# A per-language adapter with residual and layer norm: every step of the plan gets its own key, and GpSimd copies some of the W1 tiles

## The chip, the cores and the metric

The kernel runs on one core of one Trainium2 chip. The metric is the device time of one execution in microseconds (us), the median of several runs. The engines of the core are named in the profile as PE (TensorE, matrix multiply), PEld (its weight load), DVE (VectorE), ACT (ScalarE), POOL (GpSimd) and SP (SyncE, which here only issues DMAs). An engine carries out its instructions strictly in the order in which the program lists them for it.

## The reference

`x` is 128 batches of 128 rows by 512 columns, float32. Each batch has a language number (`itok`, below 9 here, ten are provided for), which selects its matrices and vectors. For every batch:

```python
h       = relu(x @ W1[lang] + b1[lang])      # 128x512 @ 512x128
adapted = h @ W2[lang] + b2[lang]            # 128x128 @ 128x512
y       = x + adapted
normed  = (y - mean(y)) * rsqrt(var(y) + 1e-05)   # over the 512 columns
out     = x + normed * gamma[lang] + beta[lang]
```

## The kernel before

**One batch.** A batch is one tile of 128 partitions by 512 columns. Its steps, each a small function:

- `load_x(g)`, SP: the DMA of x for a group of four batches (`xp`, 4 buffers).
- `transpose_x(b)`, PE: four 128x128 transposes of x into one PSUM tile; `copy_xT(b)`, ACT: that tile to SBUF. For a batch of turn "F" four DMAs (`load_blocks`, SP) and one VectorE transpose (`turn_blocks`) do this instead, and W1 comes with four DMAs from HBM (`load_rows`).
- `stage_w1(b)`, ACT: copies the batch's W1 (128x512) out of a table of all languages in SBUF into a tile at a fixed place (`wp`, 7 buffers). For a batch of turn "w" a DMA fetches W1 from HBM by its number instead (`load_late`, SP).
- `down(b)`, PE: four matmuls with W1, recorded as eight instructions; `relu(b)`, ACT: adds b1; `up(b)`, PE: the matmul with W2 into a PSUM tile `y` (five buffers).
- `add_b2(b)`, POOL: r = x + b2 (`rp`, 4 buffers). It is there for batches of kind "P". For kind "E" there is none; instead `seed(b)`, ACT, copies x into the PSUM tile, and `up` adds onto it. For some early batches VectorE adds b2 (`vector_b2`).
- `add_beta(b)`, POOL: o = x + beta (`op`, 8 buffers for a pair of batches each).
- `residual(b)`, DVE: y = y + r with the row sums (y + b2 for "E"); `square(b)`, ACT: sum of squares about the mean; per pair of batches `scalar_means` and `deviation` on ACT and three `rstd` steps on DVE; `scale(b)`, DVE: (y - mean) * gamma; `finish(b)`, DVE: o = y * rstd + o; `store(g)`, SP: the DMA of a pair to HBM.

**The order.** `keep` ties each instruction to the one before it on its engine, so the order of the calls is the order of every queue. An opening (L605 to L644) and an epilogue for batches 116 to 127 (L708 to L858) are written out by hand. The opening ends with GpSimd's `add_beta` of batches 0 to 3. Between them stands the plan: L651 to L703 give every step a key, and L705 sorts by key and calls the steps. A key is the batch number plus an offset that is the same for all batches of a stage: `BATCH` and `PAIR` from batch 26 on, `BATCH_EDGE` and `EDGE` before it and in the last four batches, all in units of a batch. The epilogue begins on GpSimd with `b2_of(121)`, `b2_of(125)`, `beta_of(122)`, `beta_of(124)`, `b2_of(122)`, `beta_of(121)`, `b2_of(123)`, and on VectorE with `rstd` and `residual(119)`; E is 123.

`KINDS` and `TURNS` repeat every 16 batches: four of 16 are "E", two of 16 "F", one of 16 "w". Over the whole run ScalarE copies W1 91 times and seeds 24 times, and GpSimd does 206 adds in the plan (117 `add_beta` and 89 `add_b2`), after four in the opening.

Of the kernel before, what the change touches and what calls it, by code (L numbers as in the profile page):

```python
# [13 lines left out]
ET = mybir.EngineType  # L14
# [3 lines left out]
G = 4  # L18
EPS = 1e-5
FIRST = 17  # L20
EARLY = 17
LATE = 17
U = 2
MIDDLE = 26
TURNED = 32
LAST = 4
KINDS = 'EPPPPPEPEPPPEPPP'
TURNS = 'TTTTFTTTTwTTFTTT'
SEEDED = 'E'
ON_GPSIMD = 'P'  # L30
BATCH = dict(turn=0.19, copy=0.16, r=-0.36, beta=-0.13, relu=1.26, w1=-0.77, up=2.66, load=-5.59, r_late=0.22)
BATCH_EDGE = dict(copy=0.2, r=0.05, r_late=1.05, beta=1.06, relu=1.3, w1=-0.6, up=2.5)
SEED = {'E': 1.69}
PAIR = dict(stat=0.22, square=0.34, means=1.98, root=1.9, scale0=3.03, n1=2.43, n2=3.115, n3=3.28, scale1=3.4, end0=3.67, end1=4.32)
EDGE = dict(stat=0.6, square=0.68, means=1.75, root=1.77, scale0=2.64, n1=2.65, n2=3.592, n3=3.62, scale1=3.64, end0=3.66, end1=4.66)


@with_exitstack
def cond_resid_kernel(ctx: ExitStack, tc: tile.TileContext, x, itok, W1, b1, W2, b2, gamma, beta, out):
# [8 lines left out]
    nc = tc.nc  # L48
    B, S, H = x.shape
    L, _, A = W1.shape  # L50
    KC = H // P
# [27 lines left out]
    E = B - 5  # L79
# [6 lines left out]
    def xb(b):  # L86
        return xs[b // G][:, b % G, :]
# [5 lines left out]
    w1 = const.tile([P, L, KC, A], FP, name="w1")  # L93
# [34 lines left out]
    parts = const.tile([P, H], BF, name="parts")  # L128
# [14 lines left out]
    lids, w1s = {}, {}  # L143
# [8 lines left out]
    def lid(b, engine):  # L152
        g = b // G
        if (g, engine) not in lids:
            loads, vals = nc.values_load_multi_w_load_instructions(
                lang[0:1, g * G : (g + 1) * G],
                engines=[engine],
                min_val=0,
                max_val=L - 1,
                skip_runtime_bounds_check_because="clamped on the chip to 0..L-1 above",  # L160
            )
            for ins in loads:
                keep(ins)
            lids[g, engine] = vals
        return lids[g, engine][b % G]
# [95 lines left out]
    xT, hT, rs, os, ys, ssqs, nmeans, rstds = {}, {}, {}, {}, {}, {}, {}, {}  # L261
    phs, pxs, sums = {}, {}, {}


    def b2_by_matmul(b):
        return b in (0, 1) or b >= B - 2

    def kind(b):
        return KINDS[b % len(KINDS)] if MIDDLE <= b < B - LAST else "-"

    def turn(b):
        return TURNS[b % len(TURNS)] if TURNED <= b < B - LAST - 2 else "-"

    def seeded(b):
        return kind(b) in SEEDED

    def b2_on_gpsimd(b):
        return kind(b) in ON_GPSIMD or kind(b) == "-" and not b2_by_matmul(b) and not b2_by_vector(b)

    def b2_by_vector(b):  # L280
        return kind(b) == "-" and (b in (2, 3, 9, 13, 17, 21) or 24 <= b < B - 8 and (b % 16 in (1, 6, 11) or b % 32 == 30))

    x2s = {}

# [32 lines left out]

    def stage_w1(b):
        w1s[b] = wp.tile([P, KC, A], FP, tag="w1s", name=f"w1s_{b}")
        src = w1.rearrange("p l k a -> p (l k a)")[:, bass.ds(lid(b, ET.Activation) * (KC * A), KC * A)]  # L320
        keep(nc.scalar.copy(w1s[b].rearrange("p k a -> p (k a)"), src))  # L321

    def transpose_x(b):
        pxs[b] = p_x.tile([P, KC, P], FP, tag="xT", name=f"pxT_{b}")
# [16 lines left out]

    def add_beta(b):
        g, j = divmod(b, 2)
        if j == 0:
            os[g] = op.tile([P, 2, H], FP, tag="o", name=f"o_{g}")
        v = lid(b, ET.Pool)
        keep(nc.gpsimd.tensor_tensor(os[g][:, j, :], xb(b), beta_b[:, bass.ds(v * H, H)], ALU.add))  # L347
# [61 lines left out]
    def square(b):  # L409

        g, j = divmod(b, 2)
        if j == 0:
# [61 lines left out]
    def on(b):  # L474
        return 0 <= b < B
# [154 lines left out]
    spread(18, nc.scalar)  # L630
    spread(19, nc.scalar)
    add_beta(0)
    add_beta(1)
    spread(20, nc.scalar)
# [13 lines left out]
    def at(when, step, *args):  # L648
        plan.append((when, len(plan), step, args))

    for b in range(B):  # L651
        when = BATCH_EDGE if kind(b) == "-" else BATCH
        if b >= 20 and b % G == 0:
            at((11 if b == 20 else b - 7) - 0.01, load_x, b // G)
        if b >= 3:
            for n, engine in ((b + 5, ET.Activation), (b + 5, ET.PE), (b + 6, ET.Pool)):
                if on(n):
                    at(b + 0.99, lid, n, engine)
        if turn(b) in "Fw":
            at(b + BATCH["load"] - 1, lid, b, ET.SP)  # L660
            at(b + BATCH["load"], load_rows if turn(b) == "F" else load_late, b)
        if turn(b) == "F":
            at(b + BATCH["load"], load_blocks, b)
            at(b + BATCH["turn"], turn_blocks, b)
        elif 5 <= b <= E - 2:
            at(b, transpose_x, b)
            at(b + when["copy"], copy_xT, b)
        if 4 <= b <= E - 3:
            at(b + (when["r"] if seeded(b) else when["r_late"]), add_b2, b)
            at(b + when["beta"], add_beta, b)  # L670
            at(b + 1.1, down, b)
            at(b + when["relu"], relu, b)
        if seeded(b):
            at(b + SEED[kind(b)], seed, b)
        if FIRST <= b <= E - 1 and turn(b) not in "Fw":
            at(b + when["w1"], stage_w1, b)
        if 2 <= b <= E - 4:
            at(b + when["up"], up, b)
# [4 lines left out]
    def at_pair(g, when, step, *args):  # L683
        if g < E // 2 - 3 or (step, *args) in begun:
            at(2 * g + 3 + when, step, *args)

    for g in range(E // 2 - 1):
        b = 2 * g
        when = EDGE if "-" in (kind(b), kind(b + 2)) else PAIR
        for j in (0, 1):  # L690
            at_pair(g, j + when["stat"] - 0.01, vector_b2, b + j)
            at_pair(g, j + when["stat"], residual, b + j)
            at_pair(g, j + when["square"], square, b + j)
        at_pair(g, when["means"], scalar_means, g)
        at_pair(g, when["root"], deviation, g)
        if b % G == 0 and on(b + G):
            at_pair(g, when["end0"] + 0.001, lid, b + G, ET.DVE)
        for n in (1, 2, 3):
            at_pair(g, when[f"n{n}"], rstd, g, n)
        for j in (0, 1):  # L700
            at_pair(g, when[f"scale{j}"], scale, b + j)
            at_pair(g, when[f"end{j}"], finish, b + j)
        at_pair(g, when["end1"] + 0.001, store, g)  # L703

    for _, _, step, args in sorted(plan, key=lambda step: step[:2]):  # L705
        step(*args)
# [10 lines left out]
    copy_xT(E - 1)  # L717
    residual(E - 4)
    square(E - 4)
    rstd(E // 2 - 3, 3)  # L720
    relu(E - 2)
# [5 lines left out]
    end_of(E - 7)  # L727
    residual(E - 3)
    stage_w1(E)
    beta_of(E - 1)  # L730
    scalar_means(E // 2 - 2)
# [10 lines left out]
    relu(E - 1)  # L742
    down(E)
    stage_w1(E + 1)
    copy_xT(E + 1)
    transpose_x(E + 2)
# [149 lines left out]
```

## Time and profile before

| | |
|---|---|
| time, median of 3 runs | 300.57 us (300.26 to 300.83) |
| the profiled execution, its time | 301.23 us |
| the profiled execution, its span | 298.8 us |
| granted TensorE clock | 0.997 |

The span runs from the first to the last instruction that the profile shows; the time has some 2.4 us around it. In the profile's rows, a group's line names the source line, engine, operation, what is written and read by the program's names, and how often; behind the bar stand the busy time, the mean duration of one in ns, and idle time of the engine ahead of them with what ended it. In a timeline, a row's first number is the start and the second the length in us; rows that follow each other directly are merged (x2, x4). Busy time is a union, and on ScalarE, VectorE and GpSimd the next instruction starts a little before the last has ended, so a price per instruction is taken from start to start where that can be read.

### The profile page before, as it was taken

The numbers are of one execution on the slowest core, as the hardware profiler recorded it, in microseconds if no ns is written. First come the engines' busy times: TensorE is split into PE (matmuls) and PEld (weight loads), VectorE is DVE, ScalarE is ACT, GpSimd is POOL, SyncE is SP. The second block draws the span as 40 slices with busy tenths as digits, with TensorE's granted clock in tenths as the row PEclk, the third lists the DMA queues.
The fourth block names the chain that finished last, engine by engine and source line by source line (L and its number), as shares of the span: only waits on it lengthen the run. The fifth ranks groups of instructions, "written<-read, shape, count | busy, mean of one in ns | idle before, by whom it ended". The sixth has DMA issues, their size and how long they took to land.

```text
span 298.8 us, 7251 instructions
## 1 busy us (share of the span) xinstructions
PE 290.7 (97%) x1783; PEld 214.7 (72%) x1783; DVE 288.9 (97%) x775; ACT 277.2 (93%) x766; POOL 277.4 (93%) x233
## 2 busy tenths in 40 slices
PE   7899999999999999999999999999999999999993
PEld 3758777777777777777777777777777777777761
DVE  6989999999999999999999999999999999999995
ACT  5868789999999999999999999999999999999983
POOL 1299998999999999999999999999999999999962
PEclk9999999999999999999999999999999999999998
DMA  6999999996799697988888887898988698894715
GB/s 233 369 393 370 342 329 396 400 325 212 270 297 328 169 378 218 321 316 284 277 280 295 275 283 256 281 300 224 356 256 269 233 313 301 250 349 163 237 73 219
DMA packets 61195, 85.48 MB, mean 286 GB/s; under 512 B 3641, under 2 KB 25156, under 8 KB 61154
## 3 DMA queue, kind: packets, MB, share of 16 engines
q1 hardware_dynamic: 61094, 84.97, 85.1%
q8 instruction: 15, 0.25, 0.3%
q14 instruction: 26, 0.21, 0.2%
q10 hardware_dynamic: 60, 0.05, 0.1%
HBM read 51.45 MB, written 33.55 MB: 284 GB/s over the span
## 4 chain that ended last, share of the span: by engine, by line
PE 81%; DVE 6%; ACT 4%; DMA 3%; issue 3%; SPq 1%; DVEq 0%; POOL 0%; ACTq 0%; POOLq 0%
PE ph L353 33%; PE py L375 26%; PE pxT L330 15%; PE py L367 7%; DMA w<-in_L_cond_W_dram 3%; DVE py L393 2%; ACT sq L416 1%; DVE o L553 1%; DVE py L459 1%; ACT w1s L321 1%; ACT xT L334 1%; SPq L173 1%; DVE n L559 0%; ACT hT L361 0%; ACT root L426 0%
## 5 line engine op out<-in xcount | busy, mean ns | idle before, releaser
L347 POOL TENSOR_TENSOR o<-x,beta_b 128x512 f32<-128x512 f32 x121 | 155.8, 1306 | 12.9 <-DVE beta_b L259 11.6
L353 PE MATMUL ph<-xT,w1s 128*128 128x128 f32 x1024 | 136.4, 276 | 0.1
L353 PEld LDWEIGHTS ph<-xT,w1s 128*128 128x128 f32 x1024 | 125.0, 192 | 8.7 <-ACT hT L361 7.0
L340 POOL TENSOR_TENSOR r<-x,b_b 128x512 f32<-128x512 f32 x89 | 116.1, 1305 | 0.0
L375 PE MATMUL py<-w,hT 128*128 x208 | 106.7, 595 | 0.7 <-DMA w<-in_L_cond_W_dram 0.7
L330 PEld LDWEIGHTS pxT<-ident,x 128*128 128x128 f32 x468 | 60.4, 150 | 60.6 <-issue 41.6
L459 DVE SCALAR_TENSOR_TENSOR py<-py,nmean,gamma_b 128x512 f32<-128x512 f32 x124 | 93.3, 753 | 0.0
L468 DVE SCALAR_TENSOR_TENSOR o<-py,rstd,o 128x512 f32<-128x512 f32 x116 | 86.8, 748 | 0.0
L416 ACT ACTIVATE sq<-py,sum 128x512 f32<-128x512 f32 x124 | 85.6, 690 | 0.7 <-DVE rstd L435 0.2
L334 ACT COPY xT<-pxT 128x512 f32<-128x512 f32 x117 | 67.8, 580 | 6.0 <-PE pxT L330 5.8
L330 PE MATMUL pxT<-ident,x 128*128 128x128 f32 x468 | 71.2, 275 | 0.9 <-ACT gamma_b L244 0.7
L393 DVE SCALAR_TENSOR_TENSOR py<-py,r 128x512 f32<-128x512 f32 x94 | 64.9, 690 | 1.4
L321 ACT COPY w1s<-w 128x512 f32 x91 | 56.7, 623 | 0.0
L361 ACT ACTIVATE hT<-ph,b1T 128x128 f32<-128x128 f32 x128 | 47.6, 372 | 5.1 <-PE ph L353 3.4
L375 PEld LDWEIGHTS py<-w,hT 128*128 128x128 f32 x208 | 31.7, 192 | 2.1 <-DMA w<-in_L_cond_W_dram 1.2
L416 ACT ACTIVATION_READ_ACCUMULATOR sq<-py,sum 128x1 f32 x124 | 25.9, 209 | 0.0
L367 PE MATMUL py<-w,hT 128*128 x48 | 25.3, 610 | 0.0
L393 DVE SCALAR_TENSOR_TENSOR py<-py,b_b 128x512 f32<-128x512 f32 x24 | 16.6, 693 | 1.5 <-PE py L367 1.4
L426 ACT ACTIVATE root<-ssq,eps 128x2 f32<-128x2 f32 x62 | 16.5, 266 | 1.5
L316 ACT COPY py<-x 128x512 f32<-128x512 f32 x24 | 14.4, 599 | 0.0
L393 DVE DVE_READ_ACCUMULATOR py<-py,r 128x1 f32 x94 | 13.2, 140 | 0.0
L407 ACT ACTIVATE nmean<-sum 128x2 f32<-128x2 f32 x61 | 11.7, 192 | 0.0
(79 smaller groups left out, 139.8 us busy)
## 6 DMA issues: line engine op xcount, KB each, us to landing
out_dram<-o SPq DMA_DIRECT2D x62, 512.0 KB, 4.0
x<-in_x_dram SPq DMA_DIRECT2D x27, 1024.0 KB, 7.7
w1s<-in_L_cond_W_dram SPq DMA_DIRECT2D x26, 256.0 KB, 7.3
x<-in_x_dram SPq DMA_DIRECT2D x10, 512.0 KB, 6.0
w1s<-in_L_cond_W_dram SPq DMA_DIRECT2D x44, 64.0 KB, 3.2
x<-in_x_dram SPq DMA_DIRECT2D x44, 64.0 KB, 2.1
w<-in_L_cond_W_dram SPq DMA_DIRECT2D x4, 640.0 KB, 8.1
w<-in_L_cond_W_dram SPq DMA_DIRECT2D x1, 1792.0 KB, 10.2
```

The source lines that it names most:

```text
L321: keep(nc.scalar.copy(w1s[b].rearrange("p k a -> p (k a)"), src))
L330: keep(nc.tensor.transpose(pxs[b][:, k, :], cols, ident))
L334: keep(nc.scalar.copy(xT[b], pxs.pop(b)))
L340: keep(nc.gpsimd.tensor_tensor(rs[b], xb(b), b2_b[:, bass.ds(v * H, H)], ALU.add))
L347: keep(nc.gpsimd.tensor_tensor(os[g][:, j, :], xb(b), beta_b[:, bass.ds(v * H, H)], ALU.add))
L353: nc.tensor.matmul(phs[b], lhsT=w1s[b][:, k, :], rhs=xT_of(b, k), start=(k == 0), stop=(k == KC - 1))
L361: keep(nc.scalar.activation(hT[b], phs.pop(b), AF.Relu, bias=b1T[:, bass.ds(lid(b, ET.Activation), 1)]))
L375: keep(nc.tensor.matmul(ys[b], lhsT=hT[b], rhs=w2[:, bass.ds(v * H, H)], start=not m, stop=True))
L393: nc.vector.scalar_tensor_tensor(ys[b], ys[b], 1.0, r, ALU.mult, ALU.add, accum_out=sum_of(b))
L416: nc.scalar.activation(sq, ys[b], AF.Square, bias=col(sums, b), scale=-float(H), accum_out=col(ssqs, b))
L459: nc.vector.scalar_tensor_tensor(ys[b], ys[b], col(nmeans, b), gamma_b[:, bass.ds(v * H, H)], ALU.add, ALU.mult)
L468: nc.vector.scalar_tensor_tensor(o, ys[b], rstds[g][:, j : j + 1], o, ALU.mult, ALU.add)
```

## The change

Three things change together.

1. `KINDS` and `TURNS` become three strings each: the first 32 batches, a round of 16 for batches 32 to 111, and the last 16. In the rounds five of 16 are "E" (four before) and none is "w"; a new turn "c" stands once in a round (at its first batch) and for batches 113, 114 and 118 to 121. In the last 16 one batch is "E" (114).
2. `stage_w1` puts the copy of W1 on GpSimd for a batch of turn "c". Batches that were "w" are now copied by ScalarE ("T") or GpSimd.
3. The offsets common to a stage are replaced by a table, `STEPS`: for every step and every batch an offset of its own (by batch for the first 32, by place in the round, by batch for the last 16). The loads of x have their own list, `X_STEPS`. So the order on every queue changes in many places, also within pairs: `scale` and `finish` of the second batch can come ahead of the first's, and stores are not in order of pairs. The steps that belong to a pair get their key from the pair's first batch, and the two tiles that a pair shares are now made by whichever batch of it comes first.

By the sorted keys GpSimd has 214 entries in the plan: 117 `add_beta`, 86 `add_b2` and 11 W1 copies; the last is `add_b2(119)`. ScalarE copies W1 86 times and seeds 27 times. The opening and the epilogue are unchanged, and so are all matmuls, sums and scalings. The core of the diff:

```diff
-MIDDLE = 26
-TURNED = 32
-LAST = 4
-KINDS = 'EPPPPPEPEPPPEPPP'
-TURNS = 'TTTTFTTTTwTTFTTT'
+KINDS = ('MMDDPPPPPDPPPDPPPDPPPDPPPPPPEPPP', 'PPEPEPPPPPEPEPEP', 'PPEPPPPPPPPPPPMM')
+TURNS = ('TTTTTTTTTTTTTTTTTTTTTTTTTTTTTTTT', 'cTTTFTTTTTTTFTTT', 'TccTFTccccTTTTTT')
...
-BATCH = dict(turn=0.19, copy=0.16, r=-0.36, beta=-0.13, relu=1.26, w1=-0.77, up=2.66, load=-5.59, r_late=0.22)
...
+STEPS = {
...
+    "r": (
...
+        (1.8, 1.88, 0, 0.78, 0, 1.26, 1.12, 0.71, 2.71, 2.56, 0, 1.16, 0, -0.64, 0, 1.21,),
+        (2.31, 3.5, 0, 5.73, 5.19, 2.55, 5.28, 28.54, -7.67, 0, 0, 0, 0, 0, 0, 0,),
+    ),
...
+}
+X_STEPS = (-7.78, -3.65, -4.39, -2.97, -1.33, -4.62, -6.08, -2.97, -1.33, -4.62, -6.08, -2.97, -1.33, -4.62, -6.08, -2.97, -1.33, -4.62, -6.08, -2.97, -1.33, -4.62, -6.08, -6.44, -6.96, -8.54, 0.77)
...
+    def of(parts, b):
+        if b < len(parts[0]):
+            return parts[0][b]
+        return parts[1][b % steady] if b < closing else parts[2][b - closing]
...
     def stage_w1(b):
         w1s[b] = wp.tile([P, KC, A], FP, tag="w1s", name=f"w1s_{b}")
-        src = w1.rearrange("p l k a -> p (l k a)")[:, bass.ds(lid(b, ET.Activation) * (KC * A), KC * A)]
-        keep(nc.scalar.copy(w1s[b].rearrange("p k a -> p (k a)"), src))
+        gpsimd = turn(b) == "c"
+        v = lid(b, ET.Pool if gpsimd else ET.Activation)
+        src = w1.rearrange("p l k a -> p (l k a)")[:, bass.ds(v * (KC * A), KC * A)]
+        dst = w1s[b].rearrange("p k a -> p (k a)")
+        keep(nc.gpsimd.tensor_copy(dst, src) if gpsimd else nc.scalar.copy(dst, src))
...
-        if j == 0:
+        if g not in os:
             os[g] = op.tile([P, 2, H], FP, tag="o", name=f"o_{g}")
...
+    def when(name, b):
+        return b + of(STEPS[name], b)
...
-            at((11 if b == 20 else b - 7) - 0.01, load_x, b // G)
+            at(b + X_STEPS[b // G - 5], load_x, b // G)
...
-            at(b, transpose_x, b)
-            at(b + when["copy"], copy_xT, b)
+            at(when("transpose", b), transpose_x, b)
+            at(when("copy", b), copy_xT, b)
...
-        at_pair(g, when["end1"] + 0.001, store, g)
+        at_pair(g, when("store", b), store, g)
```

More of the change, by code (lines that the diff above doesn't have):

```diff
@@ L22 @@
 LATE = 17
-U = 2
-MIDDLE = 26
-TURNED = 32
-LAST = 4
-KINDS = 'EPPPPPEPEPPPEPPP'
-TURNS = 'TTTTFTTTTwTTFTTT'
+KINDS = ('MMDDPPPPPDPPPDPPPDPPPDPPPPPPEPPP', 'PPEPEPPPPPEPEPEP', 'PPEPPPPPPPPPPPMM')
+TURNS = ('TTTTTTTTTTTTTTTTTTTTTTTTTTTTTTTT', 'cTTTFTTTTTTTFTTT', 'TccTFTccccTTTTTT')
 SEEDED = 'E'
 ON_GPSIMD = 'P'
-BATCH = dict(turn=0.19, copy=0.16, r=-0.36, beta=-0.13, relu=1.26, w1=-0.77, up=2.66, load=-5.59, r_late=0.22)
[L32 to L35, printed above, removed]
+STEPS = {
+    "load": (
[3 rows of a table added]
+    ),
+    "transpose": (
[3 rows of a table added]
+    ),
+    "turn": (
[3 rows of a table added]
+    ),
+    "copy": (
[3 rows of a table added]
+    ),
[4 rows of a table added]
+    ),
+    "down": (
[3 rows of a table added]
+    ),
+    "relu": (
[3 rows of a table added]
+    ),
[4 rows of a table added]
+    ),
+    "beta": (
[3 rows of a table added]
+    ),
+    "seed": (
[3 rows of a table added]
+    ),
[4 rows of a table added]
+    ),
[4 rows of a table added]
+    ),
+    "stat": (
[3 rows of a table added]
+    ),
+    "square": (
[3 rows of a table added]
+    ),
+    "means": (
[3 rows of a table added]
+    ),
+    "root": (
[3 rows of a table added]
+    ),
+    "scale": (
[3 rows of a table added]
+    ),
[4 rows of a table added]
+    ),
[4 rows of a table added]
+    ),
[4 rows of a table added]
+    ),
+    "end": (
[3 rows of a table added]
+    ),
+    "store": (
[3 rows of a table added]
+    ),
+}
+X_STEPS = (-7.78, -3.65, -4.39, -2.97, -1.33, -4.62, -6.08, -2.97, -1.33, -4.62, -6.08, -2.97, -1.33, -4.62, -6.08, -2.97, -1.33, -4.62, -6.08, -2.97, -1.33, -4.62, -6.08, -6.44, -6.96, -8.54, 0.77)
 @with_exitstack
@@ L262, in cond_resid_kernel, with kind, turn @@
     phs, pxs, sums = {}, {}, {}
-    def b2_by_matmul(b):
[L266 to L272, printed above, removed]
+    steady = len(KINDS[1])
+    closing = B - len(KINDS[2])
+    def of(parts, b):
+        if b < len(parts[0]):
+            return parts[0][b]
+        return parts[1][b % steady] if b < closing else parts[2][b - closing]
+    def kind(b):
+        return of(KINDS, b)
+    def turn(b):
+        return of(TURNS, b)
+    def b2_by_matmul(b):
+        return kind(b) == "M"
     def seeded(b):
@@ L277, in b2_on_gpsimd @@
     def b2_on_gpsimd(b):
-        return kind(b) in ON_GPSIMD or kind(b) == "-" and not b2_by_matmul(b) and not b2_by_vector(b)
+        return kind(b) in ON_GPSIMD
     def b2_by_vector(b):
-        return kind(b) == "-" and (b in (2, 3, 9, 13, 17, 21) or 24 <= b < B - 8 and (b % 16 in (1, 6, 11) or b % 32 == 30))
+        return kind(b) == "D"
     x2s = {}
@@ L411, in square @@
         g, j = divmod(b, 2)
-        if j == 0:
+        if g not in ssqs:
             ssqs[g] = st.tile([P, 2], FP, tag="ssq", name=f"ssq_{g}")
@@ L649, in at @@
         plan.append((when, len(plan), step, args))
+    def when(name, b):
+        return b + of(STEPS[name], b)
     for b in range(B):
-        when = BATCH_EDGE if kind(b) == "-" else BATCH
         if b >= 20 and b % G == 0:
-            at((11 if b == 20 else b - 7) - 0.01, load_x, b // G)
+            at(b + X_STEPS[b // G - 5], load_x, b // G)
         if b >= 3:
@@ L658, in cond_resid_kernel @@
                     at(b + 0.99, lid, n, engine)
-        if turn(b) in "Fw":
-            at(b + BATCH["load"] - 1, lid, b, ET.SP)
-            at(b + BATCH["load"], load_rows if turn(b) == "F" else load_late, b)
         if turn(b) == "F":
-            at(b + BATCH["load"], load_blocks, b)
-            at(b + BATCH["turn"], turn_blocks, b)
+            at(when("load", b) - 1, lid, b, ET.SP)
+            at(when("load", b), load_rows, b)
+        if turn(b) == "F":
+            at(when("load", b), load_blocks, b)
+            at(when("turn", b), turn_blocks, b)
@@ L665, in cond_resid_kernel @@
         elif 5 <= b <= E - 2:
-            at(b, transpose_x, b)
-            at(b + when["copy"], copy_xT, b)
+            at(when("transpose", b), transpose_x, b)
+            at(when("copy", b), copy_xT, b)
         if 4 <= b <= E - 3:
[L669 to L672, printed above, removed]
+            if b2_on_gpsimd(b):
+                at(when("r", b), add_b2, b)
@@ L673, in cond_resid_kernel @@
+            at(when("beta", b), add_beta, b)
+            at(when("down", b), down, b)
+            at(when("relu", b), relu, b)
         if seeded(b):
-            at(b + SEED[kind(b)], seed, b)
-        if FIRST <= b <= E - 1 and turn(b) not in "Fw":
-            at(b + when["w1"], stage_w1, b)
+            at(when("seed", b), seed, b)
+        if FIRST <= b <= E - 1 and turn(b) != "F":
+            at(when("w1", b), stage_w1, b)
         if 2 <= b <= E - 4:
-            at(b + when["up"], up, b)
+            at(when("up", b), up, b)
@@ L680, in cond_resid_kernel, with at_pair @@
     begun = [(step, n) for n in (E - 7, E - 6, E - 5) for step in (vector_b2, residual, square)]
     begun += [(scalar_means, E // 2 - 3), (deviation, E // 2 - 3), (scale, E - 7), (rstd, E // 2 - 3, 1)]
-    def at_pair(g, when, step, *args):
+    def at_pair(g, key, step, *args):
         if g < E // 2 - 3 or (step, *args) in begun:
-            at(2 * g + 3 + when, step, *args)
+            at(key, step, *args)
     for g in range(E // 2 - 1):
         b = 2 * g
[L689 to L695, printed above, removed]
-        if b % G == 0 and on(b + G):
[L697 to L702, printed above, removed]
-        at_pair(g, when["end1"] + 0.001, store, g)
@@ new lines, in cond_resid_kernel @@
+        for n in (b, b + 1):
+            if b2_by_vector(n):
+                at_pair(g, when("vb2", n), vector_b2, n)
+            at_pair(g, when("stat", n), residual, n)
+            at_pair(g, when("square", n), square, n)
+        at_pair(g, when("means", b), scalar_means, g)
+        at_pair(g, when("root", b), deviation, g)
+        for n in (1, 2, 3):
+            at_pair(g, when(f"n{n}", b), rstd, g, n)
+        for n in (b, b + 1):
+            at_pair(g, when("scale", n), scale, n)
+            at_pair(g, when("end", n), finish, n)
@@ L705, in cond_resid_kernel @@
+        if b % G == 0 and on(b + G):
+            at_pair(g, when("scale", b) + 0.001, lid, b + G, ET.DVE)
+        at_pair(g, when("store", b), store, g)
     for _, _, step, args in sorted(plan, key=lambda step: step[:2]):
```

70 rows, old and new, of the table STEPS are left out of this document.

## The prediction, made before the changed kernel was run

> **What bounds the kernel now.** I read the page's head, then the stages, then the chain of waits, then each engine's timeline at the two ends.
>
> ```profile
> span 298.8 us, 7251 instructions
> ...
> PE 290.7 (97%) x1783; PEld 214.7 (72%) x1783; DVE 288.9 (97%) x775; ACT 277.2 (93%) x766; POOL 277.4 (93%) x233
> ```
>
> Four engines are over 90% busy, so the average does not tell which one sets the end. The stages say more:
>
> ```profile
> core 0: us, PE busy (x) PEld busy (x) DVE busy (x) ACT busy (x) POOL busy (x), PEclk, DMA share, GB/s
> ...
> 75.00:110.00 35.00, 35.00 (x221) 26.09 (x219) 34.47 (x91) 34.45 (x97) 35.00 (x29) 1.00 0.86 281
> ...
> 145.00:180.00 35.00, 35.00 (x221) 26.18 (x220) 34.62 (x93) 34.45 (x98) 35.00 (x30) 1.00 0.87 285
> ...
> 280.00:290.00 10.00, 10.00 (x61) 7.18 (x61) 9.74 (x32) 9.08 (x27) 8.15 (x7) 1.00 0.22 84
> ```
>
> GpSimd (POOL) is busy all 35 of 35 us in the steady stage; TensorE looks the same, but its ends are modelled, so I take it from the chain, where a row is the start of one batch's `down`:
>
> ```profile
> 97.64 0.89 PE ph L353 x8
> 99.83 0.89 PE ph L353 x8
> ...
> 104.21 0.89 PE ph L353 x8
> 105.97 0.89 PE ph L353 x8
> ...
> 140.56 0.89 PE ph L353 x8
> ```
>
> An ordinary batch takes TensorE 99.83 - 97.64 = 2.19 us, an "F" batch, which has no TensorE transpose, 105.97 - 104.21 = 1.76. Sixteen batches with two F would take 14 x 2.19 + 2 x 1.76 = 34.18; they took 140.56 - 105.97 = 34.59. So TensorE is within 0.41 us per 16 batches of what its instructions need: all that a better order can win in five such rounds is 2.1 us, and about 0.25 in the closing batches.
>
> Now GpSimd, whose rows I count:
>
> ```profile
> 13.07 4.98 POOL L347 TENSOR_TENSOR o<-x,beta_b 128x512 f32<-128x512 f32 x4 [11.61 <-DVE beta_b L259]
> 18.00 1.27 POOL L340 TENSOR_TENSOR r<-x,b_b 128x512 f32<-128x512 f32 x1
> ...
> 45.10 1.30 POOL L340 TENSOR_TENSOR r<-x,b_b 128x512 f32<-128x512 f32 x1
> 47.68 2.51 POOL L347 TENSOR_TENSOR o<-x,beta_b 128x512 f32<-128x512 f32 x2 [1.29 <-DMA out_dram<-o]
> ...
> 271.96 1.33 POOL L347 TENSOR_TENSOR o<-x,beta_b 128x512 f32<-128x512 f32 x1
> 273.20 2.56 POOL L492 TENSOR_TENSOR r<-x,b_b 128x512 f32<-128x512 f32 x2
> ...
> 280.61 2.54 POOL L492 TENSOR_TENSOR r<-x,b_b 128x512 f32<-128x512 f32 x2
> ```
>
> Four adds stand in the opening, 206 in the plan, and the epilogue's begin at 273.20. 273.20 - 13.07 less the one wait (47.68 - 45.10 - 1.23 = 1.35) is 258.8 us for 210 adds: **1.232 us from start to start, with no other gap**. (18.00 - 13.07 over 4 gives the same 1.23.) GpSimd never catches up and never rests. It is a queue in fixed order, so whatever is added to it before a given add delays that add by its full length. What it feeds at the end:
>
> ```profile
> 274.81 0.70 DVE L393 SCALAR_TENSOR_TENSOR py<-py,r 128x512 f32<-128x512 f32 x1
> ...
> 283.62 0.69 DVE L393 SCALAR_TENSOR_TENSOR py<-py,r 128x512 f32<-128x512 f32 x1
> ...
> 295.12 0.87 DVE L553 SCALAR_TENSOR_TENSOR o<-n,rstd_of,base 128x256 f32<-128x256 f32 x2
> ```
>
> These are the `residual` of batch 119 (E-4), of 123 (E), and the last arithmetic. VectorE is 9.74 of 10 us busy from 280 to 290, so behind residual 119 lies 21.2 us of nearly solid VectorE work, which I let shrink by 0.3 at most. `b2_of(E)`, the add that residual 123 needs, starts at 280.61 and ends 1.23 later, 1.8 us ahead of use. That 1.8 is all the room GpSimd has.
>
> **The change part by part.** *GpSimd's sum.* Counted off the two tables: seeds go from 24 to 27 (5 of 16 in the five steady rounds, 1 instead of 3 in batches 112 to 123), so the plan has 3 fewer `add_b2`: -3 x 1.232 = -3.7 us. W1 copies on GpSimd: five in the rounds (batches 32 to 96) and 113, 114, 118 to 121: +11 c, c being a 128x512 f32 copy on GpSimd. Plan entries on this queue: 206 become 214. Sorting the keys puts `add_b2(119)` last of them, directly ahead of the epilogue. It ends at 273.20 - 3.7 + 11 c = 269.5 + 11 c, if the wait of 1.35 stays (batch 17's output buffer still needs the first store, and SP's queue is the same up to there). Residual 119 started at 274.81, so
>
> the end moves by 269.5 + 11 c - 274.8 - 0.3 = **11 c - 5.6**.
>
> *The price c.* No copy runs on GpSimd before. The near rows:
>
> ```profile
> 0.75 0.20 POOL L119 MEMSET ones<- 128x128 bf16 x1 [0.29 <-POOLq L882]
> 0.89 0.20 POOL masks.py:197 MEMSET ident<- 128x128 f32 x1
> 1.03 0.10 POOL L123 MEMSET eps<- 128x1 f32 x1
> 1.17 0.29 POOL masks.py:199 TENSOR_SCALAR_AFFINE_SELECT ident<-ident 128x128 f32<-128x128 f32 x1
> ```
>
> Below: a memset only writes; 128 columns cost 1.03 - 0.89 = 0.14 us to the next start, of which 0.03 is fixed if scaled from the one-column ones; four times 0.11 plus 0.03 is 0.47. Above: the affine select reads one operand and writes one, 0.29 against 0.10 for one column, so 0.10 + 4 x 0.19 = 0.86 long, 0.8 from start to start if it overlaps as the adds do (1.30 long, 1.232 apart); it also computes a mask. Far above: an add, 1.232, with twice the reading. A copy lies between the memset and the select; I take **0.6**, nearer the memset because nothing is computed. 11 c is then 6.6, the end +1.0; with 0.47 -0.4, with 0.8 +3.2, with 1.232 +8.0.
>
> The Trainium skill, GPSIMD Engine Reference, section 4.1 (Engine selection), calls one-input work on GpSimd roughly line-rate; at its 1.2 GHz that is an estimate of 0.43 us for 512 elements and, with a fixed part like the adds', 0.57, by which the end would move +0.7. The same page, section 3.1 (Elementwise), gives about 1.8 cycles per element and 769 ns for 512 elements as a tight loop's best; by that it would be +2.9. No run here shows either yet; the memset row agrees with the first, the select row with the second.
>
> *ScalarE.* In a round of 16 it gains one seed and no W1 copy is saved (one moves to GpSimd, but the by-id load becomes a copy):
>
> ```profile
> L321 ACT COPY w1s<-w 128x512 f32 x91 | 56.7, 623 | 0.0
> ...
> L316 ACT COPY py<-x 128x512 f32<-128x512 f32 x24 | 14.4, 599 | 0.0
> ```
>
> So up to +0.6 us a round on an engine with (35 - 34.45) = 0.55 us idle in 35; between 0 and 0.6, and in the closing it is freed of five copies (3.1 us). That can eat the 0.41 a round that TensorE could win. It costs the end nothing as long as GpSimd is the later one; without that cover it would cost at most 5 x 0.2. VectorE keeps its instructions, in another order. TensorE's `up` moves behind the next transpose in part of each round: the same instructions, nothing.
>
> *SP's queue.* Six by-id loads of W1 go, and nothing waited for them on the path above. The loads of x change place: group 6 is now behind store 6, whose pair ends with `finish(13)`.
>
> ```profile
> 43.04 3.44 SPq L472 DMA_DIRECT2D out_dram<-o  x3
> 46.59 0.94 SPq L83 DMA_DIRECT2D x<-in_x_dram  x1
> 49.63 4.44 SPq L472 DMA_DIRECT2D out_dram<-o  x2
> ...
> 52.92 0.74 DVE L468 SCALAR_TENSOR_TENSOR o<-py,rstd,o 128x512 f32<-128x512 f32 x1
> ```
> ```profile
> DMA to landing us min/median/max: 9.9/11.2/12.5
> ```
> ```profile
> 62.13 0.60 PE L330 MATMUL pxT<-ident,x 128*128 128x128 f32 x4
> ```
>
> Before, group 6 was issued at 46.59. Behind `finish(13)`, which ended at 53.66 and now stands one residual and one scale (about 1.3 us) earlier, it goes out near 53. In that stretch a group took 9.9 to 12.5 us, but the queue is emptier by then, so 7 to 10: it lands at 60 to 63. GpSimd wants it for `add_b2(24)`, which by the new table stands behind 38 adds: 13.07 + 38 x 1.232 + 1.35 = 61.2; TensorE wants it at 62.13. So GpSimd stalls 0 to 1.8 us, each of which goes to the end in full. At the other end `add_b2(120)` is put ahead of those of 112 to 119 and holds one of the four `r` buffers until its residual, so that two of these adds may wait for a residual before them: from nothing to one residual's 0.7 us. For both together, 0 to 2.5, I take +0.5: the load is likelier to be in time than not, and the `r` waits shrink if VectorE is early.
>
> **Sum:** 11 x 0.6 - 5.6 = +1.0, with the stalls **+1.5**. (At residual 123 the same comes out: 6.6 - 3.7 - 1.8 of room = +1.1.) The profiled execution took 301.23 for a span of 298.8; its own forecast is 302.7, and the median of the runs, 0.66 below it, goes from 300.57 to **302.1**.
>
> **The rivals.** *A, GpSimd's copy is hidden (faster).* If consecutive copies and adds overlap so that c is below 0.45, the eleven copies cost less than the three adds and the room give, GpSimd is no longer the later one, and TensorE's 0.41 a round comes through. From 0.45 down it decides; at c = 0.3 it is 3.3 - 5.6 = -2.3, which is also TensorE's limit of 2.1 + 0.25. In the middle, at 0.38: 300.57 - 1.4 = 299.2. For it: GpSimd has 0.64 us less to do in each steady round even at 0.6. Against it: the memset, which does not even read, scales to 0.47.
>
> *B, no change.* c from 0.45 to 0.55 and little stalling: 11 x 0.5 - 5.6 + 0.2 = +0.1, 300.7. For it the memset's rate; against it that a read must be waited for.
>
> *C, the copy runs like the affine select or worse.* c = 0.8 to 1.0: +3.2 to +5.4, with the stalls 303.8 to 306.5; I take 304.5. For it, the select is the only GpSimd row that reads one operand. Against it, the select also works out a mask. By the Trainium skill's GPSIMD Engine Reference, section 3.1, the time would be near here, 300.57 + 2.9 + 0.5 = 304.0.
>
> *D, the table doesn't keep the engines fed:* out-of-order stores hold an output buffer, or a W1 copy on GpSimd waits for a free W1 buffer, and GpSimd stops once a round for some 0.6 us: five rounds, +3. Against it: each round frees GpSimd of 0.64 us, and the only buffer wait before is the one of 1.35. It is counted with C.
>
> **How the numbers follow.** Forecast (c 0.55 to 0.75) 0.40; C with D 0.22; B 0.20; A 0.18. A measurement of this kernel tells from no change about 0.2%, 0.6 us: slower is the forecast and C, 0.62; same is B, 0.20; faster is A, 0.18. The range leaves out the lower half of A and the upper third of C: 299.5 to 305.3. The forecast's own range is 301.0 to 303.6.
>
> **What would show it.** Right: GpSimd's timeline without gaps from 47 to about 284 except near 61; copies of 0.55 to 0.75 from start to start; the residuals of 119 and 123 released by GpSimd's `r`, over a us later than 274.81 and 283.62; TensorE's rounds at 34.2 to 34.5, and its lead then lost in the last 25 us. Wrong: `r` of batch 119 ready long before its residual; c at 0.45 or less; or a stall elsewhere that is larger than GpSimd's lateness.

## The result and the profile after

| | before | after |
|---|---|---|
| median of the runs, us | 300.57 (300.26 to 300.83) | 304.06 (303.55 to 304.92) |
| profiled execution, us | 301.23 | 303.55 |
| its span, us | 298.8 | 301.8 |

The changed kernel is slower: a ratio of 1.0123 (95% interval 1.0102 to 1.0144), 3.5 us by the medians, 3.0 by the spans. (The profiled execution has 2.4 us around its span before and 1.8 after, so I compare spans and not its times.) I had forecast +1.5. The five runs of the changed kernel lie 1.4 us apart: the two with a granted clock of 1.00 took 303.55 and 303.84, the three with 0.992 to 0.996 took 304.06 to 304.92, and what makes the difference stays open.

GpSimd first, by its groups of instructions (busy time, mean ns of one, idle time before them), and by all its waits (total, times, longest):

```profile
L436 POOL COPY w1s<-w 128x512 f32 x11 | 7.0, 646 | 0.0
```
```profile
POOL o L462 <- DVE beta_b L363: 11.6, 1, 11.6
POOL r L455 <- DMA x<-in_x_dram: 1.7, 1, 1.7
POOL o L462 <- DMA out_dram<-o: 1.2, 1, 1.2
```

The eleven copies are there, and one wait is new: 1.7 us for a load of x. GpSimd's timeline shows where, and what a copy costs from one start to the next:

```profile
252.50 1.27 POOL L455 TENSOR_TENSOR r<-x,b_b 128x512 f32<-128x512 f32 x1 [1.71 <-DMA x<-in_x_dram]
253.72 0.60 POOL L436 COPY w1s<-w 128x512 f32 x1
254.29 1.26 POOL L455 TENSOR_TENSOR r<-x,b_b 128x512 f32<-128x512 f32 x1
...
268.93 1.16 POOL L436 COPY w1s<-w 128x512 f32 x2
270.06 6.18 POOL L462 TENSOR_TENSOR o<-x,beta_b 128x512 f32<-128x512 f32 x5
276.21 1.26 POOL L455 TENSOR_TENSOR r<-x,b_b 128x512 f32<-128x512 f32 x1
277.43 2.48 POOL L607 TENSOR_TENSOR r<-x,b_b 128x512 f32<-128x512 f32 x2
```

A copy takes 254.29 - 253.72 = **0.57 us** of the queue. The add that waits at 252.50 is `add_b2(120)`, put ahead of those of 112 to 119: it is the first to need the x group of batches 120 to 123. SP issued that load 9.5 us earlier than before, but not early enough for this add (the first row is the changed kernel, the second the kernel before):

```profile
245.15 0.38 SPq L187 DMA_DIRECT2D x<-in_x_dram  x1
```
```profile
254.67 0.96 SPq L83 DMA_DIRECT2D x<-in_x_dram  x1
```

The last add of the plan, `add_b2(119)`, stands behind two copies and five `add_beta` and ends at 277.43. VectorE's timeline (the wait in brackets) shows its residual waiting for just that, at 277.50 where it was 274.81:

```profile
277.50 0.70 DVE L508 SCALAR_TENSOR_TENSOR py<-py,r 128x512 f32<-128x512 f32 x1 [1.35 <-POOL r L455]
```

Only 1.35 of these 2.7 us is the wait for GpSimd: without it VectorE would have come to this residual at 276.15, 1.3 us later than before. The chain of waits that ended last leads over GpSimd from 264.00 on to this residual; the steps up to it are:

```profile
271.29 4.95 POOL o L462 x4
276.24 1.24 POOL r L455
...
277.50 0.07 DVE py L508
```

From 265 to 280 the table by stages (before, then after) has GpSimd busy throughout, and in the changed kernel the three others are idle for 2.2 to 5.4 us:

```profile
265.00:280.00 15.00, 15.00 (x97) 11.32 (x96) 14.89 (x42) 14.50 (x40) 15.00 (x13) 1.00 0.71 243
```
```profile
265.00:280.00 15.00, 12.65 (x77) 9.13 (x76) 12.81 (x34) 9.63 (x29) 15.00 (x15) 1.00 0.85 273
```

GpSimd's sum closes on these rows: its epilogue begins at 273.20 (before) + 11 x 0.57 - 3 x 1.232 + 1.7 = 277.5, against 277.43 seen.

Now the steady rounds. In the chain of waits a row is the start of a batch's `down`:

```profile
123.27 0.89 PE ph L468 x8
...
132.02 0.89 PE ph L468 x8
...
134.36 0.75 DVE o L583
...
135.15 1.12 PE py L490 x2
136.71 0.89 PE ph L468 x8
...
157.73 0.89 PE ph L468 x8
```

A round is 157.73 - 123.27 = 34.46 us, 0.13 less than before. It is the 34.18 of the instructions plus one batch that is 0.31 late: two batches take 4.69 instead of 4.38 between 132.02 and 136.71, where `up` waits for a y tile that VectorE's `finish` (134.36) frees.

### The profile page after: what moved, and what is told of

Its sections match the earlier page's. It is cut to its first block, busy times and chain, and to the rows that moved or that the text cites. A ratio compares the mean times of both kernels' runs of the same rounds, so it can differ in the third digit from the quotient of the medians.

```text
span 301.8 us, 7204 instructions
## 1 busy us (share of the span) xinstructions
PE 290.9 (96%) x1783; PEld 217.2 (72%) x1783; DVE 290.5 (96%) x775; ACT 274.2 (91%) x764; POOL 279.8 (93%) x241
## 4 chain that ended last, share of the span: by engine, by line
PE 75%; DVE 9%; POOL 5%; issue 5%; DMA 3%; SPq 1%; ACT 1%; DVEq 0%; POOLq 0%; ACTq 0%
PE ph L468 30%; PE py L490 23%; PE pxT L445 14%; PE py L482 8%; POOL o L462 3%; DMA w<-in_L_cond_W_dram 3%; DVE py L508 2%; DVE py L574 2%; DVE o L583 2%; DVE o L668 1%; POOL r L455 1%; SPq L277 1%; DVE n L674 0%; POOL w1s L436 0%; DVE part L547 0%
## 5 line engine op out<-in xcount | busy, mean ns | idle before, releaser
L462 POOL TENSOR_TENSOR o<-x,beta_b 128x512 f32<-128x512 f32 x121 | 154.7, 1323 | 12.8 <-DVE beta_b L363 11.6
L468 PEld LDWEIGHTS ph<-xT,w1s 128*128 128x128 f32 x1024 | 129.1, 192 | 33.1 <-ACT hT L476 24.0
L455 POOL TENSOR_TENSOR r<-x,b_b 128x512 f32<-128x512 f32 x86 | 111.6, 1322 | 1.7 <-DMA x<-in_x_dram 1.7
L583 DVE SCALAR_TENSOR_TENSOR o<-py,rstd,o 128x512 f32<-128x512 f32 x116 | 84.1, 746 | 0.6
L445 PEld LDWEIGHTS pxT<-ident,x 128*128 128x128 f32 x468 | 58.9, 150 | 34.7 <-issue 23.0
L449 ACT COPY xT<-pxT 128x512 f32<-128x512 f32 x117 | 69.0, 589 | 8.9 <-PE pxT L445 8.5
L508 DVE SCALAR_TENSOR_TENSOR py<-py,r 128x512 f32<-128x512 f32 x91 | 63.0, 692 | 2.3 <-POOL r L455 1.4
L436 ACT COPY w1s<-w 128x512 f32 x86 | 53.3, 625 | 0.2 <-issue 0.2
L508 DVE SCALAR_TENSOR_TENSOR py<-py,b_b 128x512 f32<-128x512 f32 x27 | 18.6, 690 | 0.0
L428 ACT COPY py<-x 128x512 f32<-128x512 f32 x27 | 16.4, 609 | 0.2
L522 ACT ACTIVATE nmean<-sum 128x2 f32<-128x2 f32 x61 | 12.9, 211 | 0.8 <-DVE py L508 0.5
```

The source lines that it names most:

```text
L436: keep(nc.gpsimd.tensor_copy(dst, src) if gpsimd else nc.scalar.copy(dst, src))
L445: keep(nc.tensor.transpose(pxs[b][:, k, :], cols, ident))
L449: keep(nc.scalar.copy(xT[b], pxs.pop(b)))
L455: keep(nc.gpsimd.tensor_tensor(rs[b], xb(b), b2_b[:, bass.ds(v * H, H)], ALU.add))
L468: nc.tensor.matmul(phs[b], lhsT=w1s[b][:, k, :], rhs=xT_of(b, k), start=(k == 0), stop=(k == KC - 1))
L508: nc.vector.scalar_tensor_tensor(ys[b], ys[b], 1.0, r, ALU.mult, ALU.add, accum_out=sum_of(b))
```

## The experiments

My theory after the result: the end follows GpSimd's queue, and the copies' sum and the stall of 1.7 make the loss. Rivals: the closing table (batches from 112 on) loses the time by its order, whatever GpSimd's work; or VectorE or ScalarE is as tight as GpSimd, so that nothing taken from GpSimd is won. All medians below stand beside the kernel before on the same chip (300.4 to 300.8).

**One stall, or six copies, taken away.** First `add_b2(120)` goes behind that of 118, so that it no longer waits for x; then the six closing copies go back to ScalarE; then both.

```diff
 "r", closing
-  (2.31, 3.5, 0, 5.73, 5.19, 2.55, 5.28, 28.54, -7.67, ...
+  (2.31, 3.5, 0, 5.73, 5.19, 2.55, 5.28, 28.54, 3.4, ...
```
```diff
-TURNS = (..., 'TccTFTccccTTTTTT')
+TURNS = (..., 'TTTTFTTTTTTTTTTT')
```

> Theory (GpSimd's queue sets the end): in the changed kernel add_b2(120) stands ahead of the adds of 112 to 119 and stood 1.71 us waiting for its group of x. Put behind add_b2(118), where the group has long landed, it waits for nothing: the last add of the plan ends 1.7 us earlier and the run takes about 302.4 us (304.06 - 1.7). Rival (the new order starves TensorE through ScalarE, 24 us of waits for hT): GpSimd's wait is hidden, the time stays at 304 within 0.4.

> The six W1 copies of the closing batches (113, 114, 118 to 121) go back to ScalarE at the same keys; the rest is the changed kernel. Theory (GpSimd's sum): six copies of 0.57 us less ahead of add_b2(119), 3.4 us; ScalarE has room there (5.7 to 8.2 busy of 10 us between 260 and 280). About 300.9 us, a little more if the copies push a relu back. Rival (ScalarE is what starves TensorE): six copies of 0.52 us more on ScalarE, 304 to 307 us.

> Both edits together. Theory: 5.1 us less on GpSimd ahead of add_b2(119), which then ends near 272.3 us, before VectorE wants it; the end is then set by TensorE and VectorE, which were 0.5 to 0.8 us ahead of the old kernel at batches 112 to 118: 299.6 to 300.4 us, that is the old kernel's time or a little under it. Rival: 304 us or more, as with the second edit alone.

Measured: 303.14, 302.81 and 302.95 (ratios 1.0085 [1.0069, 1.0102], 1.0077 [1.0060, 1.0094], 1.0088 [1.0071, 1.0105]). All three fall short of what the theory gives. GpSimd's waits show what came in place of the stall; the first kernel has no wait for x left to speak of, but

```profile
POOL r L455 <- DVE py L508: 1.4, 2, 1.2
```

and the second, with 3.4 us less to do,

```profile
POOL r L455 <- DMA x<-in_x_dram: 2.8, 1, 2.8
...
POOL r L455 <- DVE py L508: 1.3, 2, 0.7
```

The third waits for r buffers alone:

```profile
POOL r L455 <- DVE py L508: 2.1, 2, 1.7
POOL r L455 <- DVE part L545: 2.0, 1, 2.0
```

Taking the stall or the work away turns it into a wait for one of the four r buffers. So removing the one visible wait doesn't remove the lost time.

**The copies in the old order.** In the kernel before, W1 of ten batches (32, 48, 64, 80, 96, 113, 114, 118, 119, 120) goes from ScalarE to GpSimd, at the old keys.

```diff
+        gpsimd = b in (32, 48, 64, 80, 96, 113, 114, 118, 119, 120)
...
-        keep(nc.scalar.copy(w1s[b].rearrange("p k a -> p (k a)"), src))
+        keep(nc.gpsimd.tensor_copy(dst, src) if gpsimd else nc.scalar.copy(dst, src))
```

> The kernel before, in its own order, with ten W1 copies put on GpSimd at their old keys (batches 32, 48, 64, 80, 96, 113, 114, 118, 119, 120; 121 keeps its by-id load). Theory: ten times 0.57 is 5.7 us more on a queue that had 1.8 us of room: 300.57 + 5.7 - 1.8 - 0.3 = 304.2 us, with no change of order at all. Rival (the order is the cost, the copies are not): 300 to 301 us, since ScalarE is relieved of ten copies.

Measured: 305.68 (1.0172 [1.0155, 1.0189]), more than the sum. The sum holds on the queue: its epilogue begins 278.68 - 273.20 = 5.5 us later, for 10 x 0.57 = 5.7. The rest goes with a wait of TensorE for the copies themselves, which come too late at the old keys:

```profile
PE ph L355 <- POOL w1s L323: 4.8, 7, 1.8
```

**Which queue's order.** Five kernels change the closing's order by parts. The first gives W1 to ScalarE and puts the adds of 117, 119 and 120 in order; the second and third go back to the old offsets for every closing step (all 0.6 later), with the old kinds and W1 on ScalarE; the third also keys one W1 copy a round behind the relu that I thought held up the late batch; the fourth has the old offsets with the changed kernel's work, all eleven copies included. The fifth changes GpSimd's queue alone, back to the fourth's.

```diff
 "r", closing, first kernel
-  (2.31, 3.5, 0, 5.73, 5.19, 2.55, 5.28, 28.54, -7.67, ...
+  (2.31, 3.5, 0, 5.73, 5.19, 4.6, 5.28, 5.6, 5.9, ...
```
```diff
 every step of the closing, second to fourth, as here "up"
-  (2.94, 3.1, 3.38, 4.71, 5.21, 6.57, 7.56, 10.6, ...
+  (3.26, 3.26, 3.26, 3.26, 3.26, 3.26, 3.26, 3.26, ...
```
```diff
 "r", closing, fifth kernel ("beta" and "w1" likewise)
-  (2.31, 3.5, 0, 5.73, 5.19, 2.55, 5.28, 28.54, -7.67, ...
+  (2.414, 1.418, 0, 6.148, 6.058, 7.568, 13.258, 80.994, 79.998, ...
```

> The changed kernel with the six closing W1 copies of GpSimd given back to ScalarE, and the keys of add_b2 for 117, 119 and 120 put back in the order of the batches (4.6, 5.6, 5.9), so that add_b2(119) stands ahead of the last five add_beta instead of behind them and no add takes an r buffer early. If GpSimd's order alone is what kept the closing late: add_b2(119) ends some 5 us earlier, residual(119) then follows TensorE, and the time is 300 to 301. If the order of VectorE's finishes and scales, which holds the y tiles, is a limit of its own: TensorE goes on waiting for y tiles, and only 0.2 to 0.5 us of 302.8 are won, about 302.5.

> The changed kernel's tables up to batch 111 and the old kernel's order from batch 112 on (old offsets for every step, all shifted alike by 0.6, the old E/P pattern, no W1 copy on GpSimd there, one by ScalarE for batch 121, the old issue points of the last four x groups). If the loss is made in the closing table alone, whichever part of it: 299.9 to 300.3, the rounds of 34.47 and the closing of before. If the steady rounds of the changed kernel leave something that comes due at the end (GpSimd later by its five copies): 5 x 0.57 less the three seeds' adds of the steady rounds... that is, GpSimd 5 x 0.57 - 5 x 1.23 = -3.3 us in the rounds, so no loss by this either.

> As the run with the old closing, and W1 of batches 58, 74, 90 and 106 keyed 0.4 later, so that ScalarE does the relu that TensorE waits for (0.31 us, once a round) ahead of that copy. If that copy is the cause of the round's 0.31: rounds of 34.15 instead of 34.47, and 4 x 0.31 = 1.2 us less than the run with the old closing, 298.7 to 299.1. If W1 then comes late for its own down: no change or some tenths more.

> The changed kernel's work throughout (its seeds and all eleven W1 copies on GpSimd) with the old kernel's order from batch 112 on, the six closing copies keyed 3 steps ahead of their batch. If the sum of GpSimd's queue is the whole loss: 11 x 0.57 - 3 x 1.23 - 1.8 us of room = +0.8, 301.0 to 301.5. If a copy ahead of time holds W1 buffers or the order of the closing costs nothing by itself: 303 to 304, as the changed kernel.

> The changed kernel with one queue changed: from batch 112 on GpSimd takes its adds and its W1 copies in the order of the run with the old order and the new work (301.40); TensorE, VectorE, ScalarE and the loads of x keep the changed kernel's order. If GpSimd's order in the closing makes the 2.7 us that lie between 301.40 and 304.06: 301.3 to 302.0. If the order of VectorE and ScalarE makes them: 303.5 to 304.1. If each makes a part: between.

Measured: 302.51, 301.51, 301.49, 301.40 (1.0027 [1.0013, 1.0041]) and 301.86 (1.0049 [1.0032, 1.0066]). The fourth has all of the changed kernel's work and loses 2.7 us less than it: **most of the loss is the closing's order**. The fifth shows that 2.2 of the 2.7 lie in GpSimd's queue alone: with its own order back it stalls no more, so the stalls belong to the order of that queue. In the fourth and the fifth GpSimd has no stall in the closing, and its epilogue begins where the sum without a stall puts it, 273.20 + 6.27 - 3.70 = 275.8; the fourth, then the fifth:

```profile
275.86 2.59 POOL L607 TENSOR_TENSOR r<-x,b_b 128x512 f32<-128x512 f32 x2
```
```profile
275.83 2.49 POOL L607 TENSOR_TENSOR r<-x,b_b 128x512 f32<-128x512 f32 x2
```

But the fifth isn't held by GpSimd any more. From 262 us on the chain that ended last has only steps of TensorE and VectorE, and residual 119 begins without a wait for GpSimd and yet 1.6 us later than before:

```profile
276.40 0.70 DVE L508 SCALAR_TENSOR_TENSOR py<-py,r 128x512 f32<-128x512 f32 x1
```

So about half of the 2.7 us by which this residual is late in the changed kernel would be there without GpSimd's lateness, which hides it. The first kernel says the same: it came out where its rival puts it (about 302.5), its residual 119 begins at 276.80 though the add for it was done by 269.4, and its adds, now in order, wait for r buffers all the same:

```profile
POOL r L455 <- DVE part L545: 1.8, 1, 1.8
POOL r L455 <- DVE py L508: 1.6, 1, 1.6
```

As I read the rows, its adds run ahead of the residuals and have to wait, while five `add_beta`, which could fill that time, stand behind them in the queue (270.06 to 276.21 in the changed kernel); in the fifth the betas stand between the adds. No run moves the betas alone, so this isn't shown.

The second and third are misses: without the six copies GpSimd's epilogue begins at 270.15, and yet nothing is won. The relu theory falls too: in the third the late batch stays at 2.50 us.

Two more runs try the counterparts: the old order everywhere but on GpSimd, and the first kernel's `r` keys alone, with the copies kept.

> The counterpart: GpSimd's closing queue in the changed kernel's order, all other queues from batch 112 on in the old order. If GpSimd's order makes the 2.7 us: 303.5 to 304.5, with the waits for r buffers and r of 119 last. If the others' order makes them: 301.3 to 302.0.

> The changed kernel with add_b2 of 117, 119 and 120 in the order of the batches and nothing else changed: the eleven W1 copies stay on GpSimd, the betas stay where they are. If the three displaced adds are the whole loss of the closing order: 301.4 to 302.0. If displaced betas and copies count as much: 302.5 to 303.2.

Measured: 309.91 (1.0292 [1.0248, 1.0336]) and 303.56 (1.0116 [1.0091, 1.0140]). The first isn't a clean counterpart, because the old issue point of the x load is later still for an early `add_b2(120)`:

```profile
POOL r L455 <- DMA x<-in_x_dram: 6.5, 1, 6.5
```

The second is above both of its forecasts. The wait for x is gone, but waits for W1 and r buffers take its place, 1.4 us for 1.7, and the epilogue begins at 277.42, as in the changed kernel:

```profile
POOL w1s L436 <- PE ph L468: 0.9, 2, 0.6
...
POOL r L455 <- DVE py L508: 0.5, 1, 0.5
```

So the adds alone don't bring the loss back. The fifth kernel above, which does, puts the adds, the betas and the copies back together; what each of them does alone isn't shown.

**Less work on GpSimd.** The seeds alone, in the kernel before; and, in the old order with the new work, the closing W1 loaded from memory, or all eleven off GpSimd (`'wTTTFTTTTTTTFTTT', 'TTTTFTTTTwTTTTTT'`).

```diff
-KINDS = 'EPPPPPEPEPPPEPPP'
+KINDS = 'PPEPEPPPPPEPEPEP'
```
```diff
-TURNS = (..., 'cTTTFTTTTTTTFTTT', 'TccTFTccccTTTTTT')
+TURNS = (..., 'cTTTFTTTTTTTFTTT', 'TwwTFTwwwwTTTTTT')
+        if turn(b) == "w":
+            at(b - 7, lid, b, ET.SP)
+            at(b - 6, load_late, b)
```

> One part of the change alone, in the kernel before: batches seeded in 5 of 16 (30 batches instead of 24 with the old periods), so GpSimd has 6 adds or 7.4 us less to do, ScalarE 6 seeds or 3.6 us more; no W1 copy on GpSimd, old keys. If GpSimd is the one limit before, the end comes earlier until TensorE's own 0.41 us per 16 batches is used up: 298.5 to 299.5. If VectorE (34.5 of 35 us busy) and ScalarE are as tight as GpSimd: 300.2 to 301.0, nothing won.

> The run with the old order and the new work (301.40), with the six closing W1 of GpSimd loaded by id from memory instead of copied, so that neither GpSimd nor ScalarE has them: GpSimd 6 x 0.57 = 3.4 us less. If GpSimd's sum is the 0.7 us: 299.7 to 300.5, with GpSimd's add for batch 121 starting near 272.4 instead of 275.86. If VectorE, which is busy 34.85 of 35 us in the rounds, or the step from one table to the other holds the end at 301.4: 301.2 to 301.6.

> The same order, no W1 copy on GpSimd at all: in the rounds W1 of 1 of 16 batches is loaded by id, in the closing ScalarE copies five and one is loaded, as before the change. GpSimd has 11 x 0.57 = 6.3 us less than in the run with the old order and the new work. If GpSimd's sum is the 0.7 us and ScalarE has room: 299.5 to 300.3. If ScalarE or VectorE holds it: 301.2 to 301.8, as the run with the old closing.

Measured: 306.18 (1.0190 [1.0173, 1.0207]), 303.63 (1.0102 [1.0081, 1.0123]) and 301.77 (1.0033 [1.0020, 1.0046]). The seeds alone (31 batches, one more than the expectation counts) cost 5.7 us at the old keys: ScalarE has seven more copies, TensorE's rounds grow from 34.59 to some 35.1, and GpSimd, with less to do, waits for r buffers; which of these lengthens the rounds isn't shown. With W1 loaded, GpSimd waits for an output buffer. On SP's queue the six early loads of W1 (L697) wait until TensorE's `down` frees a tile, and the stores stand behind them:

```profile
POOL o L462 <- DMA out_dram<-o: 4.7, 2, 4.5
```
```profile
SPq L697 <- PE ph L468: 9.5, 6, 3.2
```

The last has 6.3 us less on GpSimd than the 301.40 kernel and isn't faster. In its closing TensorE waits for ScalarE's relu and seed (weight loads at the step from the rounds to the closing):

```profile
250.80 0.97 PEld L468 LDWEIGHTS ph<-xT,w1s 128*128 128x128 f32 x8 [0.77 <-ACT hT L476]
...
263.88 0.30 PEld L482 LDWEIGHTS py<-w,hT 128*128 128x128 f32 x2 [1.00 <-ACT py L428]
```

The 301.40 kernel has the same wait for the seed (0.71 us of TensorE there, 0.81 here). So there is a second limit near 301.5 for the new rounds with an old closing, and the 0.7 us of the 301.40 kernel can't be given to GpSimd alone; whether that seed is the limit isn't shown. The changed order throughout, with its six closing W1 loaded, was tried too; in that order the queues wait for each other in a circle, so it has no time.

**GpSimd by itself.** Two last kernels add to the one before nothing but copies on GpSimd into a tile that nobody reads, three (keyed as shown) and eight of them (batches 36, 45 and so on to 99).

```diff
+    def idle_copy():
+        t = tp.tile([P, KC * A], FP, tag="spare", name="spare", bufs=1)
+        keep(nc.gpsimd.tensor_copy(t, w1.rearrange("p l k a -> p (l k a)")[:, : KC * A]))
...
+    for b in (40, 60, 80):
+        at(b + 0.5, idle_copy)
```

> The kernel before with three more 128x512 copies on GpSimd, among batches 40 to 80, into a tile that nobody reads: 3 x 0.57 = 1.7 us more on its queue, all else as before. By GpSimd's sum and the room of 1.8: no change, 300.4 to 300.9. If GpSimd has no room: +1.7, 302.3. If the copies slow VectorE, which shares the stretch: more than 0.3 even here.

> The same with eight such copies among batches 36 to 99: 4.6 us on GpSimd's queue. By the sum and the room of 1.8: +2.8, 303.2 to 303.7, with GpSimd's add for batch 121 starting at 277.8. If GpSimd is not what sets the end: no change, 300.4 to 300.9. If there is no room: +4.6, 305.2.

Measured: 300.60 (0.9997 [0.9988, 1.0006]) and 303.33 (1.0097 [1.0082, 1.0112]). Both as GpSimd's sum and its room say. The epilogue of the first, then of the second, and in the second the residual of 123, which waits for GpSimd:

```profile
274.95 2.52 POOL L496 TENSOR_TENSOR r<-x,b_b 128x512 f32<-128x512 f32 x2
```
```profile
277.52 2.51 POOL L496 TENSOR_TENSOR r<-x,b_b 128x512 f32<-128x512 f32 x2
```
```profile
286.23 0.70 DVE L397 SCALAR_TENSOR_TENSOR py<-py,r 128x512 f32<-128x512 f32 x1 [0.50 <-POOL r L496]
```

The kernels side by side: the begin of GpSimd's epilogue (273.20 before), and what the time would be if each us past 273.20 + 1.8 = 275.0 went to the end:

| kernel | epilogue begins, us | 300.6 + what is past 275.0 | measured, us |
|---|---|---|---|
| three idle copies | 274.95 | 300.6 | 300.60 |
| eight idle copies | 277.52 | 303.1 | 303.33 |
| old order, new work | 275.86 | 301.5 | 301.40 |
| GpSimd's order old | 275.83 | 301.4 | 301.86 |
| W1 on ScalarE, three adds in order | 276.73 | 302.3 | 302.51 |
| closing W1 on ScalarE | 276.77 | 302.4 | 302.81 |
| W1 on ScalarE, `add_b2(120)` late | 276.85 | 302.5 | 302.95 |
| closing W1 loaded | 276.99 | 302.6 | 303.63 |
| `add_b2(120)` late | 277.95 | 303.6 | 303.14 |
| three adds in order | 277.42 | 303.0 | 303.56 |
| changed kernel | 277.43 | 303.0 | 304.06 |
| ten copies, old order | 278.68 | 304.3 | 305.68 |
| old closing, W1 on ScalarE | 270.15 | 300.6 | 301.51 |
| no W1 copy on GpSimd | 272.61 | 300.6 | 301.77 |

The rule holds to 0.6 us in eight of the eleven kernels in which GpSimd begins late. The ten copies are 1.4 above it, where TensorE waits for the copies. The changed kernel and the one with W1 loaded are each 1.0 above it by their medians; their profiled executions, from which the begins are read, took 303.55 and 302.66, 0.5 and 0.1 above. A fit doesn't prove the cause: with GpSimd's order old, the chain shows that GpSimd isn't what holds the end. The last two rows are the second limit.

## Why the prediction was right or wrong

*GpSimd sets the end: right for GpSimd's lateness, but with another limit close behind.* The chain of the changed kernel leads over GpSimd's closing. Eight copies that nobody reads cost 2.6 us (303.33 - 300.78, the kernel before beside it), three cost nothing. The room of 1.8 us, read off one pair of rows, was right to about 0.2. What I didn't see is the limit behind it: with GpSimd's stalls gone the time is 301.40 to 301.86, and with less work on GpSimd besides it is no shorter (301.49 to 301.77).

*The copy's price: right within 0.03.* 0.57 against 0.60; 11 c is 6.3 instead of 6.6. By the Trainium skill, GPSIMD Engine Reference, section 4.1 (Engine selection), one-input work is about line-rate; the 0.57 estimated from it with a fixed part agrees with the trace, though I had read that fixed part (0.14) off no row. The 769 ns of its section 3.1 (Elementwise) isn't what a plain copy takes here. That the median, 304.06, falls on the 304.0 that rival C gives by that price is a coincidence: the copy is not its cause. (C's lower bound leaves the stalls out; with them it is 304.3 and not 303.8.) *The three adds fewer: right.*

*The stalls: the step that failed.* The term for the stalls was mis-sized: I put "+0.5" for both, and 1.7 was measured. I had named a wait for group 6 near 61 us as the one to look for; that load was issued at 53.52, about as I had worked out, and nothing waited for it. The stall came at the other end, 1.7 us at 252.50: I had seen that `add_b2(120)` is put ahead of those of 112 to 119, but priced only the r buffer that it holds, not the load of its own x. And it isn't one mishap: with that wait removed some 1.4 us appear at r buffers (1.4) or W1 and r buffers (0.9 + 0.5), until GpSimd's closing is put back in order (301.86). D, the rival nearest to this, has it as a stall "once a round" for an output or a W1 buffer, and I counted it with another; the steady rounds have no such stall, and in the closing it was x and r, and W1 in one run.

*The tail: right for VectorE, but something behind it was left out.* I let VectorE's work behind residual 119 shrink by 0.3. Residual 119 is 2.7 us later, and VectorE's last instruction, at 295.12 before, 2.5 us later:

```profile
297.62 0.87 DVE L668 SCALAR_TENSOR_TENSOR o<-n,rstd_of,base 128x256 f32<-128x256 f32 x2
```

So that part shrank by 0.2. The span grew by 3.0: the other 0.5 lies behind VectorE's last instruction, where the last stores took 2.4 to 3.1 us to land instead of 1.7. Why they took longer stays open. Added up against the spans: -0.3 for the copies, +1.2 for the stall, +0.1 for VectorE's tail and +0.5 for the stores bring the forecast's +1.5 to the +3.0 seen.

*TensorE's rounds: inside the range I gave (34.2 to 34.5), near its upper end.* A y tile that VectorE frees late keeps 0.3 of the 0.41 in four rounds. The small lead was lost by the closing, as forecast.

## What to carry to other kernels

When an engine with a fixed order never rests, its queue can be summed row by row, and here the sum foretold where it ends to 0.3 us; adding work that nobody reads measures the room that it has. When a change reorders that queue, follow each displaced instruction to every resource that it now needs early (its load, its buffer) and to every one behind it: removing only the wait that the profile shows may move it to the next buffer. A limit found this way says what more work costs, and not what less work wins, because the next engine may stand right behind it.

## What the runs showed of the hardware

A GpSimd copy of 128x512 float32 takes 0.57 us of its queue, under half of an add of the same size (1.23), though it is recorded 0.6 to 0.8 long. A late start of GpSimd costs little here: where its first wait was 12.7 us instead of 11.6, the wait for the first store was shorter, 0.4 or less instead of 1.1 to 1.7 (0.9 in one run).
